# A graph layer that gathers its neighbours: each list gather counts itself when issued, and waits for the count of those ahead

## The chip, the cores and the metric

The kernel runs on one core of a Trainium2 chip. Four engines compute: TensorE (PE), VectorE (DVE), ScalarE (ACT) and GpSimd (POOL); SyncE (SP) issues the plain transfers. GpSimd issues the indirect transfers, those whose rows are picked by a list of indices. The metric is the device time of one execution in microseconds; the number given is the median of the runs.

## The reference, cut to what matters

There are 16 graphs of 1024 nodes with 64 features each and an adjacency matrix for each graph. Per graph, features are normalised and clipped at zero. Nodes with more than ten neighbours lose some edges by a rule on the rank of each neighbour. Then every node takes three quantiles over its remaining neighbours (itself among them), channel by channel, adds their weighted sum to its own features, and a small two-layer network follows.

```python
h = jnp.maximum(_layernorm(x, axis=-1), 0.0)
# inside the layer, x is h
rem = neigh & (sk > 1) & (rank % sk == sk - 1) & mask[:, :, None]
rem = rem | jnp.swapaxes(rem, 1, 2)
adj_d = jnp.where(rem, 0.0, adj_)
nd = adj_d > 0
vals = jnp.where(nd[..., None], x[:, None, :, :], jnp.inf)
s = jnp.sort(vals, axis=2)
...                                   # quantiles 0.25, 0.5, 0.75 with weights 0.25, 0.5, 0.25
out = (1.0 + EPS_GIN) * x + agg
h = jax.nn.relu(out @ W1 + b1)
y = h @ W2 + b2
return y * mask[..., None].astype(y.dtype)
```

The layer's result is added to the original `x`.

## The kernel before

Graphs are worked on in pairs, eight pairs in all. For one graph b, `load` (line 894) brings in the adjacency matrix in eight blocks of 128 rows and turns it into 0/1 form; `number`, `drop` and `keep` find which edges stay; `order` ranks the nodes by their number of neighbours, so that nodes with many stand in the first of eight tiles; `collect` (line 1069) makes, for each node, the list of its neighbours' row numbers, in the tile `idx` (written for the last time at line 1134). `normalize` writes the normalised features to a table in HBM, `gtab`.

`fetch` (line 1263) then gathers. One list gather is one indirect transfer: for one slot s of one tile k it brings 128 rows of 64 floats, one row for each node of the tile, from `gtab` into a slot of the tile `g` of its class. There are four classes of tiles (`CLASSES`: tile 0; tiles 1 to 3; 4 and 5; 6 and 7); classes with tiles 0 to 3 have two buffers, the other two have one. A pair has at most 126 such gathers, the last pair fewer, since part of its lists is fetched by matrix products (`pick`, line 1313). There are 952 list gathers in all. `fetch_group` (line 1606) issues 30 more indirect transfers for the few nodes with very long lists, and `scatter` (line 1688) four that write results; the change does not touch these.

`aggregate` (line 1435) sorts the gathered slots by a network of minima and maxima on DVE (lines 1376 to 1384), weights them, and adds them up on PE (line 1405). It reads the `g` tiles, so a later gather into the same buffer must wait for it. `mlp` is the small network.

The kernel's text creates the instructions in one order, and `arrange` (line 643) makes another. It takes each instruction as a step with an estimated cost, works out which steps must precede which, and runs a list scheduler: at each point the engine that is free first takes the earliest step that is ready. The result is one sequence for each engine, fixed when the program is built. Waits between engines are put in afterwards by the framework. Every indirect transfer adds 16 to one of eight semaphores when its data has landed, and the ninth waits on the semaphore of the first, and so on; so at most eight are under way.

In the built program, an instruction carries one wait. Where it has to wait for more, EventSemaphore instructions stand in front of it on the same engine, which do nothing but wait, for one or two semaphores each.

GpSimd runs its sequence in order. It has 986 indirect transfers in it, and they come in some twenty bursts: at the head of each stands a gather that waits for its list (`idx`, from DVE), or for the buffers of `g` (from PE, ACT and DVE).

The lines around the change:

Of the kernel before, what the change touches and what calls it, by code (L numbers as in the profile page):

```python
# [639 lines left out]
        return 480, 1500 + by / 300  # L640


def arrange(tc, runs, loose, tails):

    steps, found, number = [], {}, {}
    for ins in list(tc.nc.cur_bb.bb.instructions):
# [58 lines left out]
    waiting, able, sequence = ({e: [] for e in ENGINES} for _ in range(3))  # L705
# [4 lines left out]
    while done < len(steps):  # L710
# [5 lines left out]
        s = steps[heappop(able[e])]  # L716
# [19 lines left out]
        for q in ENGINES:  # L736
            while waiting[q] and waiting[q][0][0] <= free[q]:
                heappush(able[q], heappop(waiting[q])[1])

    for steps in sequence.values():  # L740
        alike = iter(sorted((i for s in steps for i in s.tail), key=lambda i: number[i.name]))
        line = [i for s in steps for i in (s.ins, *(next(alike) for _ in s.tail))]
        at = {ins.name: k for k, ins in enumerate(line)}
        for ins in line:
            if ins.name in loose and at[loose[ins.name]] < at[ins.name] - 1:
                tc.declare_no_dep(ins, loose[ins.name], reason="read in order by one engine")
        for ins, then in zip(line, line[1:]):
            tc.add_manual_dep(
                then, ins.name, mybir.DependencyInfo(mybir.DependencyClass.NoSync, mybir.DependencyReason.DATA),
                reason="order of the engine",  # L750
            )
# [3 lines left out]
def list_layer(  # L755
# [14 lines left out]
    nc = tc.nc  # L770
# [8 lines left out]
    runs = []  # L779
# [15 lines left out]
    loose, tails = {}, {}  # L795
# [95 lines left out]
    lists, owns, coefs, tables = {}, {}, {}, {}  # L891
# [348 lines left out]

    queue = deque()
    turn = [0]

# [9 lines left out]
    def opening(some, m=B // 2 - 1):  # L1255

        tiles, slots = some
        if (m, tiles) not in gathered:
            gathered[m, tiles] = wk.tile(
                [P, PLANS[slots][0], len(tiles), 2, C], F32, name=f"g{tiles[0]}", bufs=2 - tiles[0] // 4  # L1260
            )

    def fetch(m, classes=CLASSES, halves=(0, 1)):

        for tiles, slots in classes:
            lo, n = tiles[0], len(tiles)
            held, order = PLANS[slots][:2]

            def begin(h, tiles=tiles, lo=lo, n=n, slots=slots, held=held):
                opening((tiles, slots), m)  # L1270
                nc.scalar.copy(gathered[m, tiles][:, slots - 1, :, h], owns[m][:, lo:lo + n, h])

            def gather(h, slot, k, at, tiles=tiles, lo=lo):
                return nc.gpsimd.indirect_dma_start(  # L1274
                    out=gathered[m, tiles][:, slot, k - lo, h], out_offset=None, in_=tables[2 * m + h][0],
                    in_offset=bass.IndirectOffsetOnAxis(ap=lists[2 * m + h][:, at:at + 1], axis=0),
                    element_offset=tables[2 * m + h][1],
                )

            for h in halves:  # L1280
                queue.append(partial(begin, h))
                for k in tiles:
                    for s, slot in enumerate(order[:FULL[k] + ((k, FULL[k]) in HOSTS)]):
                        if m < pairs - 1 or s >= LEAST[k]:
                            queue.append(partial(gather, h, slot, k, PASSED[k] + s))
# [149 lines left out]
    def aggregate(m, o, between=None):  # L1435
# [4 lines left out]
        for half in (0, 1) if last else (1, 0):  # L1440
            parts = CLASSES[2 * half:2 * half + 2][::1 if last else -1]
            for sides in ((0, 1), (1, 2)) if last and half else ((0, 2),):
# [47 lines left out]
                if half and not last:  # L1490
                    for h in ((0, 1),) if m < pairs - 2 else ((0,), (1,)):
                        fetch(m + 1, CLASSES[2:], halves=h)
# [272 lines left out]
    late_constants()  # L1765
    drain(ahead, drop(0), normalize(0), keep(0), order(0), collect(0, ((0, 1), (1, NT))))
    fetch(0, halves=(0,))
    issue()
    drain(load(1), prepare(1))
    fetch(0, halves=(1,))  # L1770
    issue()
    for m in range(pairs + 1):
# [22 lines left out]
                next(side)  # L1795
        weave(chain(results(m - 1) if m else (), (1.0,)), 140.0 if m else 1.0, side, 85.0 if m < pairs - 1 else 45.0)

    arrange(tc, runs, loose, tails)


def ones_col(pool, nc):
# [68 lines left out]
@with_exitstack  # L1870
def quantile_graph_layer(
    ctx: ExitStack,
    tc: tile.TileContext,
    x: bass.AP,
    adj: bass.AP,
    nodemask: bass.AP,
    W1: bass.AP,
    b1: bass.AP,
    W2: bass.AP,
    b2: bass.AP,  # L1880
    cbf: bass.AP,
    cf32: bass.AP,
    ci32: bass.AP,
    out: bass.AP,
):
    keep = ctx.enter_context(tc.tile_pool(name="keep", bufs=1))
    flag = keep.tile([1, 1], I32, name="flag")
    list_layer(tc, x, adj, nodemask, W1, b1, W2, b2, cbf, cf32, out, flag)
    full = tc.nc.values_load(flag[0:1, 0:1], min_val=0, max_val=1)
    with tc.If(full > 0):  # L1890
        dense_layer(tc, x, adj, nodemask, W1, b1, W2, b2, cbf, cf32, ci32, out)
# [83 lines left out]
```

## Time and profile before

| | |
|---|---|
| runs | 1517.57 us median of 3 (1513.0 to 1521.52) |
| profiled execution | 2610.97 us, of which the span from first to last instruction is 2609.2 us |
| busy in the span | DVE 1224.7 us, PE 1220.6, ACT 1111.4, POOL 966.4 |
| list gathers (line 1274) | 952, 921.0 us busy, 967 ns on average, 942 to 1491 |
| other indirect transfers | 26 and 4 at lines 1624 and 1628, 4 at line 1691: 33.2 us busy |
| granted clock of PE | 0.709 of full speed |
| moved by DMA | 121.62 MB, 47 GB/s |

Busy time is the time in which an engine has at least one instruction in work; waiting, branches and the sequencer's own work are not in it. [...] The profiled execution is a run with recording on, and it took 1.72 times as long as the runs without; so its durations of single instructions can be used, but its sums of idle time have to be read with care.

### The profile page before, as it was taken

How to read it: one execution, taken by the hardware profiler on the slowest of the kernel's cores; microseconds unless marked ns; L12 is line 12 of the kernel's file. 1: busy time of each engine (PE TensorE's matmuls, PEld its weight loads, DVE VectorE, ACT ScalarE, POOL GpSimd, SP SyncE). 2: the span in 40 equal slices, each digit the busy share in tenths (PEclk: the TensorE clock that was granted, in tenths of full speed). 3: DMA queues.
4: the chain of work that ended last, by engine and by line, in shares of the span. 5: the costliest groups of instructions: out<-in, count | busy, mean ns of one | idle time of the engine just before them, and what ended most of it. 6: DMA issues, size and time to landing. Idle time of an engine off the chain costs nothing.

```text
span 2609.2 us, 29583 instructions
## 1 busy us (share of the span) xinstructions
PE 1220.6 (47%) x8971; PEld 756.3 (29%) x8971; DVE 1224.7 (47%) x5963; ACT 1111.4 (43%) x3089; POOL 966.4 (37%) x995
## 2 busy tenths in 40 slices
PE   6144246154807192253816427145392254655536
PEld 4133134032404151142413214033251122353223
DVE  5123168043508371383507704088374171449496
ACT  6244146143606271343606626055482254315355
POOL 1724431653272527324370154702507434420400
PEclk9567578576958595585957758577596566876668
DMA  5222122121213121221212112121212010100100
GB/s 171 62 77 68 39 56 73 33 58 45 56 34 86 28 70 32 62 52 50 59 26 80 42 19 59 26 65 33 51 54 50 16 21 16 32 13 3 22 9 11
DMA packets 128826, 121.62 MB, mean 47 GB/s; under 512 B 95730, under 2 KB 96274, under 8 KB 128658
## 3 DMA queue, kind: packets, MB, share of 16 engines
q1 hardware_dynamic: 97106, 87.29, 11.3%
q0 software_dynamic: 31552, 32.36, 6.4%
q8 instruction: 72, 1.18, 0.2%
q14 instruction: 96, 0.79, 0.1%
HBM read 108.79 MB, written 9.05 MB: 45 GB/s over the span
## 4 chain that ended last, share of the span: by engine, by line
another core or an unknown queue 27%; PE 17%; ACT 17%; issue 16%; DVE 6%; DMA 0%; DVEq 0%; ACTq 0%
PE codeP L1090 3%; PE acc L1405 3%; ACT dist L993 2%; ACT g L1399 2%; ACT kept L1016 2%; ACT sg L906 2%; DVE g L1384 1%; ACT ne L926 1%; PE tp L913 1%; DVE g L1379 1%; PE rk L988 1%; PE rk L983 1%; PE got L1341 1%; ACT waste L1188 1%
## 5 line engine op out<-in xcount | busy, mean ns | idle before, releaser
L1274 POOL DMA_INDIRECT g<-gtab,idx x952 | 921.0, 967 | 1373.9 <-issue 307.7
L1384 DVE TENSOR_TENSOR g<-g 128x256 f32<-128x256 f32 (+1 forms) x675 | 312.0, 484 | 39.0 <-remote 26.6
L1379 DVE TENSOR_TENSOR g<-g 128x256 f32<-128x256 f32 (+1 forms) x675 | 312.8, 486 | 28.8 <-remote 18.9
L993 ACT ACTIVATE dist<-rk,bias 128x512 f16<-128x512 f32 x256 | 170.2, 696 | 314.4 <-remote 215.0
L983 PE MATMUL rk<-kb,cnt 128*128 128x512 bf16 x256 | 121.4, 474 | 349.0 <-ACT dist L993 166.9
L926 ACT ACTIVATE ne<-tp 128x512 fp8e4<-128x512 f32 x248 | 141.0, 605 | 280.3 <-remote 226.3
L994 DVE TENSOR_SCALAR rem<-dist,half 128x1024 bf16<-128x1024 f16 x128 | 63.0, 493 | 402.6 <-ACT dist L993 351.7
L913 PE MATMUL tp<-kb,sg 128*128 128x128 bf16 x1024 | 118.4, 258 | 285.2 <-ACT sg L906 114.7
L988 PEld LDWEIGHTS <-ne 128*128 128x128 fp8e4 x1024 | 97.7, 117 | 414.4 <-issue 396.9
L1090 PE MATMUL codeP<-pack,perm 128*128 128x332 bf16 x1024 | 195.1, 333 | 11.2 <-DVE perm L1065 8.7
L913 PEld LDWEIGHTS <-sg 128*128 128x128 bf16 x1024 | 89.5, 118 | 309.0 <-issue 172.1
L1016 ACT ACTIVATE kept<-kp 128x512 fp8e4<-128x512 f32 x224 | 134.2, 615 | 91.8 <-remote 54.1
L1405 PE MATMUL acc<-g,kf 128*128 128x128 f32 (+2 forms) x472 | 141.2, 432 | 64.5 <-ACT g L1399 45.3
L1399 ACT ACTIVATE g<-g,coef 128x64 f32<-128x64 f32 x560 | 147.5, 350 | 52.2 <-DVE g L1379 21.0
L801 DVE MEMSET pause<- 128x1 bf16 x2237 | 132.0, 59 | 7.0 <-issue 7.0
L988 PE MATMUL rk<-kw,ne 128*128 128x128 fp8e5 x1024 | 128.7, 258 | 0.0
L906 ACT ACTIVATE sg<-at 128x1024 bf16<-128x1024 f32 x121 | 126.5, 1070 | 3.4 <-DMA at<-in_adj_dram 3.4
L1105 DVE MAX8 keys<-codeP 128x8 f32<-128x128 f32 x128 | 38.0, 297 | 186.7 <-ACT own L1100 145.1
L1090 PEld LDWEIGHTS <-perm 128*128 128x128 bf16 x1024 | 97.2, 105 | 89.3 <-DVE perm L1065 25.1
L1511 DVE TENSOR_SCALAR at_p<-iota,node 128x512 bf16<-128x512 f16 x208 | 66.8, 357 | 100.0 <-remote 57.4
L1019 PE MATMUL code<-kw,kept 128*128 128x17 fp8e5 x1024 | 65.5, 173 | 98.9 <-issue 56.6
L1405 PEld LDWEIGHTS acc<-g,kf 128*128 128x128 f32 x472 | 83.4, 218 | 90.0 <-ACT g L1399 57.1
(205 smaller groups left out, 2533.5 us busy)
## 6 DMA issues: line engine op xcount, KB each, us to landing
at<-in_adj_dram SPq DMA_DIRECT2D x122, 512.0 KB
g<-gtab,idx POOLq DMA_INDIRECT x952
xt<-in_x_dram SPq DMA_DIRECT2D x16, 256.0 KB
y<-in_x_dram SPq DMA_DIRECT2D x16, 256.0 KB
gtab<-xt SPq DMA_DIRECT2D x16, 256.0 KB
out_dram<-y SPq DMA_DIRECT2D x14, 256.0 KB
spare<-in_adj_dram SPq DMA_DIRECT2D x6, 512.0 KB
gg<-g SPq DMA_DIRECT2D x32, 48.0 KB
```

What stands on the lines that cost most here:

```text
L906: nc.scalar.activation(sg, at, AF.Sign)
L913: run.append(nc.tensor.matmul(tp[:, s], sg[:, m * P:(m + 1) * P], ident16, start=(s == 0), stop=(s == 3 and t // 4 != n), skip_group_check ...
L926: nc.scalar.activation(to, tp, AF.Relu, saturate=False)
L988: run.append(nc.tensor.matmul(rk[:, s * P:(s + 1) * P], ne[:, 4 * n + s, ts], upper, start=False, stop=(s == 3), skip_group_check=True,))
L993: nc.scalar.activation(dist[:, n * HALF:(n + 1) * HALF], rk, AF.Abs, bias=bias[:, t:t + 1])
L1016: nc.scalar.activation(kept[:, 4 * n:4 * n + 4], kp, AF.Relu, saturate=False)
L1090: run.append(nc.tensor.matmul(flat, perm[:, t, k * P:(k + 1) * P], pack[:, t], start=False, stop=(t == NT - 1), skip_group_check=True,))
L1274: return nc.gpsimd.indirect_dma_start(out=gathered[m, tiles][:, slot, k - lo, h], out_offset=None, in_=tables[2 * m + h][0], in_offset=bas ...
L1379: nc.vector.tensor_tensor(at(f + k * df, df, many), pa, pb, OP.min if what == "<" else OP.max)
L1384: nc.vector.tensor_tensor(pa if back else pb, pa, pb, OP.max if what == "<" else OP.min)
L1399: nc.scalar.activation(v[:, i, j], v[:, i, j], AF.Copy, scale=w[:, i, j:j + 1])
L1405: nc.tensor.matmul(acc, ident32, lines[:, s], start=False, stop=(s == now[-1] and not ends), skip_group_check=True)
```

## The change

One semaphore, `issued`, is allocated. Each list gather adds one to it when GpSimd has finished with the instruction[...]; the data may land later. After the scheduler has fixed GpSimd's sequence, `arrange` walks over the list gathers in that sequence and makes the gather with number k (counted from zero, from the third on) wait until the semaphore has reached k - 1: all gathers in front of it but the last have been issued. Nothing else changes: data, sizes and the order of the instructions on all engines stay as they are.

```diff
-def arrange(tc, runs, loose, tails):
+def arrange(tc, runs, loose, tails, paced):
...
+    for k, s in enumerate(s for s in sequence["POOL"] if s.ins.name in paced[1]):
+        if k > 1:
+            paced[1][s.ins.name].wait_op(paced[0], k - 1, "sem-ge")
     for steps in sequence.values():
...
+    paced = nc.alloc_semaphore("issued"), {}
     queue = deque()
...
+            issued, given_out = paced
+
             def gather(h, slot, k, at, tiles=tiles, lo=lo):
-                return nc.gpsimd.indirect_dma_start(
+                ins = nc.gpsimd.indirect_dma_start(
                     out=gathered[m, tiles][:, slot, k - lo, h], out_offset=None, in_=tables[2 * m + h][0],
                     in_offset=bass.IndirectOffsetOnAxis(ap=lists[2 * m + h][:, at:at + 1], axis=0),
-                    element_offset=tables[2 * m + h][1],
+                    element_offset=tables[2 * m + h][1], engine_sem=issued,
                 )
+                given_out[ins.ins.name] = ins
+                return ins
...
-    arrange(tc, runs, loose, tails)
+    arrange(tc, runs, loose, tails, paced)
```

In the built program, 950 gathers wait on `issued`. The wait takes the one place that an instruction has, so what the gather waited on before moves into EventSemaphore instructions in front of it; GpSimd has 136 of these before and 1048 after.

## The prediction

> **What bounds the kernel now.** I read the totals of the engines first, then the row of the list gathers, then GpSimd in order of time.
>
> The head of the page, with its second part's rows for the two engines that matter here:
>
> ```profile
> span 2609.2 us, 29583 instructions
> ...
> PE 1220.6 (47%) x8971; PEld 756.3 (29%) x8971; DVE 1224.7 (47%) x5963; ACT 1111.4 (43%) x3089; POOL 966.4 (37%) x995
> ...
> DVE  5123168043508371383507704088374171449496
> ...
> POOL 1724431653272527324370154702507434420400
> ```
>
> Two things stand out. Four engines are busy for about the same time, 966 to 1225 us. And the profiled execution took 2610.97 us where the runs have a median of 1517.57: the slices say where the rest is, since where POOL has a 7, DVE has a 0 or 1. The table of stretches shows one long run of gathers (565 to 600) beside a stretch without any; its columns are length, then busy time of PE, weight loads, DVE, ACT and POOL, clock and DMA:
>
> ```profile
> 565.00:600.00 35.00, 0.40 (x2) 0.00 (x0) 0.00 (x0) 0.00 (x0) 26.50 (x28) 0.56 0.14 26
> ...
> 200.00:223.00 23.00, 16.60 (x136) 11.11 (x135) 17.34 (x83) 14.60 (x46) 0.00 (x0) 1.00 0.27 81
> ```
>
> While gathers are issued back to back, PE, DVE and ACT nearly stand still, in the profiled execution. The plain runs can hold little of that: they are 1093 us shorter, and at 1517 us the three engines must be working through the gathers. So I take the rates of single instructions from this trace, and not its idle times.
>
> The gathers' own rate is in their group row and in order of time (start, duration, and in brackets the idle time before):
>
> ```profile
> L1274 POOL DMA_INDIRECT g<-gtab,idx x952 | 921.0, 967 | 1373.9 <-issue 307.7 <-ACT o L1418 307.7 <-DVE idx L1134 251.0
> ```
>
> ```profile
> 223.11 0.95 POOL L1274 DMA_INDIRECT g<-gtab,idx  x1 [74.28 <-DVE idx L1134]
> 224.36 0.95 POOL L1274 DMA_INDIRECT g<-gtab,idx  x1 [0.30 <-issue]
> ...
> 549.63 0.95 POOL L1274 DMA_INDIRECT g<-gtab,idx  x1 [0.30 <-issue]
> 550.89 1.28 POOL L1274 DMA_INDIRECT g<-gtab,idx  x1 [0.30 <-issue]
> ```
>
> A gather takes 0.946 us beside an idle DVE and, over the 149 gathers beside which DVE was busy at least 80% of the time, 1.064 on average; 0.305 us lie between two, whatever they waited for. In a plain run DVE is busy some 80% (1224.7 of 1517), so one gather costs about 1.25 to 1.37 us, and the 986 indirect transfers 1234 to 1350. Before the first stand 69.7 us and after the last 57 (2609.2 less 2552.3). That leaves 41 to 157 us of the median for waits at the heads of the 20-odd bursts. GpSimd is therefore the bound or next to it: what is added to every gather shows nearly in full, what is added at a burst's head in part.
>
> [...] the first gather's record starts at 69.74 and its last semaphore increment comes at 72.1, 1.2 us after the record's end. [...]
>
> **The change, part by part.** The order of instructions is the same on all engines, and the waits of PE, ACT, DVE and SP are the same too. On POOL, 952 gathers get an increment, 950 a wait on the new semaphore. An instruction holds one wait, so what it held before goes into an EventSemaphore ahead of it: 136 become 1048.
>
> *The new wait.* Gather k may go when k-2 is issued[...]. It has the 1.25 us of k-1 to arrive. What GpSimd's sequencer must do in that time: one EventSemaphore, 0.086 us from one to the next in a row of them at 1957.5; the gather itself, 0.52 to 0.57 us from the EventSemaphores before it to those behind it (two cases there); and from the release of a wait to the start of the gather 0.26 us (below). Together 0.9 us, less than 1.25: hidden under gather k-1, and the spacing stays. The cover is gone only if a gather became shorter than 0.9 us, or the increment came more than some 0.35 us late.
>
> *The EventSemaphores.* 912 times 0.086 us is 78 us of the sequencer's time, all in that cover. In the trace 36 indirect transfers already have EventSemaphores ahead of them inside a burst, up to four, and 35 of them start 0.305 us after their predecessor like the rest.
>
> *The heads of the bursts.* Here there is no gather to hide under. Queued behind a waiting head are only the other gathers; for these wait the sorts of the next pair. Before, the last wait of a head stood in the gather itself[...]. From the release to the start it took 0.26 us at 15 heads: idx is written at 222.58 + 0.27 and the gather starts at 223.11.
>
> ```profile
> 222.58 0.27 DVE L1134 SCALAR_TENSOR_TENSOR idx<-bit,low 128x104 int32<-128x104 f32 x1
> ```
>
> Now this wait is in an EventSemaphore[...]. Five heads (at 1485.38, 1809.93, 2123.63, 2210.87 and 2406.43) already end their wait in an EventSemaphore: from PE's increment to the start 0.727 us each, 0.697 of it behind the EventSemaphore. So 15 heads lose 0.47 us, 7.0 us, and the five pay one more EventSemaphore, 0.09 each, 0.4 us. At most 7.5 us.
>
> *The increment.* No row shows a gather with one. It costs nothing if it goes out while the next begins (the matrix engine and DVE do so hundreds of times)[...]. It can't make a gather shorter, but fewer waiting gathers could help others, which is the second rival. I take nothing.
>
> *Sum.* In the profiled execution 7.5 us at most, 2611 to 2618. In the runs a head counts where GpSimd really waits there; I take two thirds, 5 us: 1517.57 + 5 = 1522.6, +0.3%.
>
> **The rivals.**
> *GpSimd takes longer per gather.* The increment, or one that arrives late, lengthens the spacing. If it came only as the data lands, 2.35 us after the start, two gathers would take 2.35 + 0.26 = 2.6 us, 1.30 instead of 1.25 each: again 0.05, and 48 us in all where GpSimd is the bound. For it: no gather with an increment is in the trace. Against it: 0.35 us of room, and with DVE busy the spacing is already 1.37. From about 0.01 us per gather, 9.5 us, it decides; 0.03 to 0.05 give 1550 to 1570.
>
> *The other engines are freed.* In the profiled execution the standstill goes with queued gathers: in burst after burst the increment of a short PE group comes 9 to 14 us after its matmuls, as if behind some ten gathers. If the cause is how many gathers stand in GpSimd's queue, two in place of six or more take most of it away. A place in the records is this wait of ACT for matmuls that had ended at 559.2:
>
> ```profile
> 600.30 0.60 ACT L926 ACTIVATE ne<-tp 128x512 fp8e4<-128x512 f32 x1 [40.93 <-remote]
> ```
>
> If a tenth to a fifth of DVE's idle 293 us in a plain run (1517.6 less 1224.7) comes of it, the gain is 29 to 58 us: 1460 to 1490. Against it: the runs are 1093 us shorter than the profiled execution, so the standstill looks like a price of recording; standstills go on 5 to 8 us behind the last gather of a burst, when nothing is queued; and a burst keeps its rate, so if the cause is the issuing itself nothing is gained. This is the rival on the other side; it decides when over 12.6 us of standstill in the runs depend on the queue.
>
> *It does nothing.* If GpSimd comes late to most heads in a plain run, even the 5 us vanish: 1517.
>
> **How the numbers follow.** A difference under 0.5% (7.6 us) can hardly be told from none here. Chances: heads delayed, with or without effect, 0.50 (1517 to 1527, likeliest 1523; about a quarter of it over 1525.2); longer spacing 0.25 (1527 to 1612, mostly 1550 to 1570); engines freed 0.20 (1460 to 1510); nothing at all 0.05. Faster: 0.20. Within: 0.37 and 0.05, 0.42. Slower: 0.13 and 0.25, 0.38. For 8 in 10 I leave out the better part of the freed engines' case and the far end of the longer spacing: 1490 to 1565. The likeliest case has 1517 to 1527 of its own.
>
> **What would show it.** In the changed kernel's trace: gathers still 0.30 us apart and 0.946 us long beside an idle DVE; heads that start 0.7 us after their release instead of 0.26; a profiled time of 2600 to 2620. Wrong would be: gaps of 0.35 or more in mid-burst (first rival), or stretches of gathers in which PE, DVE and ACT work (second), with a profiled time hundreds of us shorter.

## The result, and the profile after

The changed kernel takes 1518.44 us (median of 12 runs, 1516.55 to 1524.3), the kernel before 1518.81 (12 runs, 1513.0 to 1524.55). The ratio is 1.0002, with a 95% interval from 0.9986 to 1.0018: no difference. Forecast were 1523 us, with 0.42 on "within 0.5%". The 5 us (+0.3%) of that forecast lie beyond the upper end of the interval.

The profiled execution is another matter: 2610.97 us before, 1518.3 after. The page of the changed kernel:

```profile
span 1516.2 us, 30478 instructions
...
PE 1124.8 (74%) x8954; PEld 711.8 (47%) x8971; DVE 1230.8 (81%) x5963; ACT 1099.1 (72%) x3089; POOL 1031.4 (68%) x995
...
DVE  5646699985899899876994689797899578998984
...
POOL 3177777677777777777777777777777777776000
...
ACT 30%; PE 23%; issue 19%; POOL 14%; DVE 10%; DMA 3%; POOLq 0%; DVEq 0%; SPq 0%; ACTq 0%
...
L1280 POOL DMA_INDIRECT g<-gtab,idx x952 | 983.5, 1033 | 347.9 <-DMA g<-gtab,idx 284.2
```

The busy times are nearly those of before (DVE 1230.8 against 1224.7, ACT 1099.1 against 1111.4), but the span is 1093 us shorter. POOL has a 7 almost everywhere, and DVE works beside it. The row of shares is the chain of work that ended last, followed back from the end: GpSimd has 14% of it. The table of stretches, for the two windows shown of before (the same times, not the same work; length, then busy time of PE, weight loads, DVE, ACT, POOL, then clock and DMA):

```profile
565.00:600.00 35.00, 24.95 (x295) 16.92 (x292) 34.89 (x193) 28.35 (x57) 27.08 (x27) 0.89 0.44 130
200.00:223.00 23.00, 11.26 (x99) 7.95 (x102) 22.03 (x102) 19.66 (x45) 17.75 (x18) 0.78 0.36 104
```

In the first, 27 gathers went out and DVE was busy for 34.89 of 35 us; before, 28 gathers went out and PE, DVE and ACT did next to nothing. I count stretches of over 3 us in which none of PE, ACT and DVE works: 71 with 747 us in all before, none after. The wait of 40.93 us on ACT, at line 926, has no successor either. What that line (now 929) waited for in the whole span, in us and times:

```profile
its engine sat idle before it (us, times) until:
  PE tp L922: 8.8, 8
  PE tp L916: 5.8, 9
```

GpSimd and one line of DVE, in order of time:

```profile
271.35 0.25 DVE L1137 SCALAR_TENSOR_TENSOR idx<-bit,low 128x104 int32<-128x104 f32 x1
272.34 1.04 POOL L1280 DMA_INDIRECT g<-gtab,idx  x1 [8.23 <-issue]
273.68 1.13 POOL L1280 DMA_INDIRECT g<-gtab,idx  x1 [0.30 <-DMA g<-gtab,idx]
...
366.23 0.94 POOL L1280 DMA_INDIRECT g<-gtab,idx  x1 [0.30 <-DMA g<-gtab,idx]
368.01 1.05 POOL L1280 DMA_INDIRECT g<-gtab,idx  x1 [0.84 <-DMA g<-gtab,idx]
369.37 1.07 POOL L1280 DMA_INDIRECT g<-gtab,idx  x1 [0.30 <-DMA g<-gtab,idx]
...
594.29 1.08 POOL L1280 DMA_INDIRECT g<-gtab,idx  x1 [0.30 <-DMA g<-gtab,idx]
595.67 1.08 POOL L1280 DMA_INDIRECT g<-gtab,idx  x1 [0.30 <-DVE g L1392]
```

Three readings. Gathers still stand 0.305 us apart (973 of the 985 gaps). The head at 272.34 starts 0.74 us after its list is written (271.35 + 0.25), not 0.26. And this is the only list gather after the first that waits for over a microsecond: from 69.5 us to the last at 1396.5, GpSimd runs through. The sum of the span is therefore 69.5 us of lead-in, 951 spacings of 1.395 us on average (32 other indirect transfers, 30 of them of `fetch_group`, are among them), and 120 us after the start of the last list gather.

So the range forecast for the runs held, and that of the profiled execution (2600 to 2620 us) failed by over 1080 us. The experiments had two questions: what makes the standstill, and what sets the time where there is none.

### The profile page after: what moved, and what is told of

The parts are those of the page before. It is cut to its first block, busy times and chain, and to the rows that moved or that the text cites. A ratio compares the mean times of both kernels' runs of the same rounds, so it can differ in the third digit from the quotient of the medians.

```text
span 1516.2 us, 30478 instructions
## 1 busy us (share of the span) xinstructions
PE 1124.8 (74%) x8954; PEld 711.8 (47%) x8971; DVE 1230.8 (81%) x5963; ACT 1099.1 (72%) x3089; POOL 1031.4 (68%) x995
## 4 chain that ended last, share of the span: by engine, by line
ACT 30%; PE 23%; issue 19%; POOL 14%; DVE 10%; DMA 3%; POOLq 0%; DVEq 0%; SPq 0%; ACTq 0%
POOL g L1280 14%; PE codeP L1093 5%; ACT dist L996 5%; PE acc L1413 5%; ACT g L1407 4%; ACT kept L1019 4%; ACT sg L909 3%; ACT ne L929 2%; DVE g L1392 2%; DVE g L1387 2%; PE tp L916 1%; ACT waste L1186 1%; ACT waste L1191 1%; PE rk L986 1%; PE rk L991 1%
## 5 line engine op out<-in xcount | busy, mean ns | idle before, releaser
L1280 POOL DMA_INDIRECT g<-gtab,idx x952 | 983.5, 1033 | 347.9 <-DMA g<-gtab,idx 284.2
L1093 PE MATMUL codeP<-pack,perm 128*128 128x332 bf16 x1024 | 182.1, 316 | 9.0 <-DVE perm L1068 8.5
L986 PE MATMUL rk<-kb,cnt 128*128 128x512 bf16 x256 | 113.1, 442 | 74.5 <-ACT dist L996 69.6
L916 PE MATMUL tp<-kb,sg 128*128 128x128 bf16 x1024 | 109.9, 246 | 72.8 <-ACT sg L909 57.5
L991 PEld LDWEIGHTS <-ne 128*128 128x128 fp8e4 x1024 | 90.7, 110 | 129.9 <-issue 107.4
L916 PEld LDWEIGHTS <-sg 128*128 128x128 bf16 x1024 | 82.6, 112 | 94.5 <-ACT sg L909 63.6
L991 PE MATMUL rk<-kw,ne 128*128 128x128 fp8e5 x1024 | 118.8, 243 | 0.0
L1098 ACT CAST st<-codeP 128x4 bf16<-128x4 f32 x128 | 21.6, 169 | 109.9 <-PE codeP L1093 109.6
L1014 PE MATMUL kp<-kw,rem 128*128 128x128 fp8e5 x1024 | 100.5, 219 | 0.0
L1009 PE MATMUL kp<-ne,kw 128*128 128x512 fp8e4 x256 | 98.7, 386 | 0.8 <-ACT dist L996 0.5
```

The lines of the kernel that those rows point to most:

```text
L916: run.append(nc.tensor.matmul(tp[:, s], sg[:, m * P:(m + 1) * P], ident16, start=(s == 0), stop=(s == 3 and t // 4 != n), skip_group_check ...
L991: run.append(nc.tensor.matmul(rk[:, s * P:(s + 1) * P], ne[:, 4 * n + s, ts], upper, start=False, stop=(s == 3), skip_group_check=True,))
L1093: run.append(nc.tensor.matmul(flat, perm[:, t, k * P:(k + 1) * P], pack[:, t], start=False, stop=(t == NT - 1), skip_group_check=True,))
L1280: ins = nc.gpsimd.indirect_dma_start(out=gathered[m, tiles][:, slot, k - lo, h], out_offset=None, in_=tables[2 * m + h][0], in_offset=bass ...
```

## The experiments

**One fact comes first, since no number below can be read without it.** The chips of these runs are of two kinds. On three of them the kernel before takes 1518 to 1522 us. On two others it takes 2624 us (24 runs, 2615 to 2635) and 2647 us (7 runs), without recording. I call them quick and stalling chips; the runs above have the times of the quick ones, though their chips are not on record. Each chip was used in one batch of runs, so whether this is a lasting property of a chip or one of that time is not shown. Each kernel is compared with the kernel before on its own chip.

| kernel | kernel before there | time | ratio, 95% interval |
|---|---|---|---|
| `count_only` | 2624.03 | 2625.95 | 1.0009 (0.9997 to 1.0021) |
| `depth8` | 2624.03 | 2634.31, one run | |
| `depth4` | 2624.03 | 2634.87, one run | |
| `depth1` | 2624.03 | 2603.62 | 0.9923 (0.9892 to 0.9954) |
| `thin_before` | 1517.89 | 1445.56 | 0.9515 (0.9484 to 0.9547) |
| `thin_after` | 1517.89 | 1448.33 | 0.9524 (0.9492 to 0.9556) |
| `after_again` | 1520.22 | 1520.18 | 0.9992 (0.9974 to 1.0011) |
| `depth1_again` | 1520.22 | 1518.88 | 0.9994 (0.9981 to 1.0008) |
| `longer` | 1520.22 | 1516.64 | 0.9983 (0.9970 to 0.9995) |
| `longer2` | 2646.74 | 2201.46 | 0.8324 (0.8297 to 0.8351) |
| `longer4` | 2646.74 | 1993.39 | 0.7525 (0.7513 to 0.7538) |
| `longer3` | 1522.18 | 1824.69 | 1.1992 (1.1972 to 1.2012) |

### Does the number of queued gathers make the standstill?

Four kernels ran on one chip. `count_only` has the increment and no wait:

```diff
-        if k > 1:
-            paced[1][s.ins.name].wait_op(paced[0], k - 1, "sem-ge")
+        pass
```

> The gathers keep their increment of the semaphore, but none waits on it. Theory (the standstill under recording comes from several gathers standing in GpSimd at once, and plain runs don't have it): profiled execution back at 2500 to 2700 us, with PE, DVE and ACT idle in the bursts; plain runs 1512 to 1525 us. Rival (the increment itself, which gives GpSimd a semaphore of its own to signal, is what ends the standstill): profiled execution stays at 1510 to 1530. Rival (a gain and a loss cancel in plain runs): without the waits the runs leave 1518 by more than 8 us.

`depth8` lets eight gathers be unissued, `depth4` four, and `depth1` only the one that waits:

```diff
-        if k > 1:
-            paced[1][s.ins.name].wait_op(paced[0], k - 1, "sem-ge")
+        if k > 7:
+            paced[1][s.ins.name].wait_op(paced[0], k - 7, "sem-ge")
```

> Gather k waits until all in front of it but the last seven have been issued. The transfers' own eight semaphores allow no more than that anyway, so the wait never holds anything back, but nearly as many EventSemaphore instructions stand on GpSimd as in the changed kernel. Theory (number of queued gathers): profiled execution 2500 to 2700 us, plain time 1512 to 1525. Rival (the EventSemaphore between two gathers gives the others room, whatever it waits for): profiled execution 1510 to 1600.

```diff
+        if k > 3:
+            paced[1][s.ins.name].wait_op(paced[0], k - 3, "sem-ge")
```

> Gather k waits until all in front of it but the last three have been issued: up to four in GpSimd instead of two. Theory: profiled execution between the two kernels' if the standstill grows with the number queued, 1600 to 2300 us; if it needs a full queue, 1510 to 1530. Plain time 1512 to 1525 in either case. Rival (EventSemaphores): 1510 to 1530 as with depth two and with depth eight.

```diff
+        if k > 0:
+            paced[1][s.ins.name].wait_op(paced[0], k, "sem-ge")
```

> Gather k waits until all in front of it have been issued: nothing runs on GpSimd while the next gather is released and started. Theory (GpSimd's spacing of gathers sets the time, and with depth two the wait lies under the gather ahead): the spacing grows from 1.34 us by the way from one gather's end to the next one's start, at least 0.26 and at most 0.73 us in place of 0.305, so by 0 to 0.43 us, likeliest 0.3; plain runs longer by 0 to 400 us, likeliest 200 to 280, and by as much as the spacing in the trace says (spacing times 950). Rival (the heads of the bursts or the other engines bound, spacing does not): with a spacing longer by 0.2 us or more the runs stay within 1% of 1518. If the spacing stays the same, the run says that the wait is not paid even without cover.

All four took 2604 to 2635 us, and so did the kernel before beside them in plain runs; of `depth8` and `depth4` there is only the profiled execution. The theory's 2500 to 2700 for the profiles of `count_only` and `depth8` was met, but not for its reason, and its range for `depth4` was missed. It also ends the statement that all these expectations shared, that plain runs don't have the standstill: 2624 us is the plain time of the kernel before on this chip. Recording doesn't make it: the profiled execution of `count_only` took 2626.54 us beside a median of 2625.95, and that of `depth1_again` below 1519.15 beside 1518.88.

The strictest of the four, `depth1`, from its page:

```profile
span 2604.6 us, 30495 instructions
...
DVE  5123168062507372192606804078375080529596
...
POOL 1724431644262416515271153700606515340500
```

and `count_only` in the table of stretches, in the window shown above for the changed kernel:

```profile
565.00:600.00 35.00, 0.00 (x0) 0.00 (x0) 0.00 (x0) 1.03 (x3) 25.75 (x28) 0.50 0.13 26
```

Where POOL has a 7, DVE has a 0 or 1, although at most one gather at a time can be in work. The stretches without PE, ACT and DVE sum to 775 us in `count_only`, 830 in `depth8`, 826 in `depth4`, 785 in `depth1`. So the number of gathers queued on GpSimd isn't the cause, and neither the increment nor the EventSemaphores are a cure. Nor is PE's lower clock, 0.705 there against 0.872 in the changed kernel's profile: its busy time is 1226.9 us in `count_only` against 1124.8, which is 102 us of some 1100. (The gap of `depth1` stays at 0.305 us: its wait costs nothing there even without cover.) What these kernels don't limit is the number of transfers that have left GpSimd and not yet landed. The 0.8% by which `depth1` is faster there stays unexplained.

### Where is the changed kernel on a stalling chip?

The changed kernel once more, without an edit:

> The changed kernel as it is. The kernel before took 2624 us on one chip, without recording, and 1518 on another; whichever of the two kinds of chip this is, the theory (the standstill belongs to the chip, and neither recording nor the number of queued gathers makes it) expects the changed kernel within 1% of the kernel before, 2600 to 2640 us or 1510 to 1526. Rival (pacing to two ends the standstill where it is): on a chip where the kernel before takes 2624 us, the changed kernel takes 1520 to 2400.

This run was on a quick chip: 1520.18 us against 1520.22. It repeats the result, but doesn't tell the rival apart. The changed kernel itself has not run on a stalling chip; depth two lies between depth one and depth four, which both stand still there, and I infer the rest.

### What does the wait cost when nothing covers it?

The edit is that of `depth1`, on a quick chip.

> Each gather waits for all in front of it. On the chip with the standstill the gap between two gathers stayed at 0.305 us. Theory (the gap of 0.305 us is itself the way from the end of one gather to the release of the next, so that a wait for the whole of it costs nothing more): gap 0.305 us, time within 0.7% of the kernel before. Rival (it has no cover and costs 0.1 us or more per gather where the other engines work): gap over 0.4 us, over 1560 us on a chip where the kernel before takes 1518.

The time is 1518.88, ratio 0.9994. The gap is 0.305 us, 973 times; theory right. GpSimd around a longer gap, in order of time:

```profile
366.95 0.94 POOL L1280 DMA_INDIRECT g<-gtab,idx  x1 [0.30 <-DMA g<-gtab,idx]
369.98 0.94 POOL L1280 DMA_INDIRECT g<-gtab,idx  x1 [2.08 <-issue]
371.22 0.95 POOL L1280 DMA_INDIRECT g<-gtab,idx  x1 [0.30 <-DMA g<-gtab,idx]
```

The semaphore records say why the gap doesn't grow: the increment of `issued` comes 10 ns after the gather's end, and the next gather starts 0.29 us after it. This is the gap itself; what GpSimd does in it is in no record.

The exception has a period. Each 106th of GpSimd's gathers is followed by a gap of about 2.09 us with depth one, and of 0.51 to 0.84 with depth two; `count_only`, `thin_before`, `depth4` and `depth8` have none. (`longer`, below, has 0.54 to 0.81 us there, with its memsets in between.) 2.09 less one gather with its gap, 1.25, is 0.84: as if something here took some 2.1 us, of which one gather ahead can cover 1.25. That it is one and the same piece of work is argued from the period and the difference; what it is, no record says. `thin_after`, below, with 144 gathers fewer, has the longer gaps at the same counts, so they go with the number of transfers and not with a place in the work. In the changed kernel this costs GpSimd 3.1 us in eight places, in `depth1_again` about 15 us in nine, and neither is seen in the runs: in `depth1_again` the last list gather starts 12.8 us later than in the changed kernel (1409.2 against 1396.5), and 108 us remain behind it instead of 120. So GpSimd has slack.

### Is GpSimd what bounds the kernel on a quick chip?

`thin_before` and `thin_after` leave 144 list gathers out:

```diff
+            def blank(h, end, tiles=tiles):
+                nc.vector.memset(gathered[m, tiles][:, 0:end, :, h], 1.0)
+
             for h in halves:
                 queue.append(partial(begin, h))
+                if tiles[0] == 6:
+                    queue.append(partial(blank, h, slots - 1))
+                    continue
```

> The kernel before, with the 144 list gathers of tiles 6 and 7 left out; their slots are filled with a constant by 16 memsets on DVE of some 0.7 us each, so sorts and sums work on other values, and the output is another. Theory (GpSimd's gathers set the time): 144 x 1.34 = 193 us less, less what DVE (1231 us busy in all, plus 11 for the memsets) then holds back: 1330 to 1400 us. Rival (the other engines or waits at the heads set the time): less than 60 us gained, over 1455 us.

It took 1445.56 us, 72 less than the kernel before: between theory (1330 to 1400) and rival (over 1455), nearer the rival. The page:

```profile
span 1442.7 us, 29324 instructions
...
PE 1118.3 (78%) x8956; PEld 703.7 (49%) x8971; DVE 1228.6 (85%) x5979; ACT 1093.2 (76%) x3089; POOL 887.0 (61%) x851
```

The last list gather starts at 1264.7 us, 132 earlier than in the changed kernel, but the end comes only 73 earlier: 178 us remain behind it instead of 120. DVE is busy 85% of the span. So gathers matter, but GpSimd alone doesn't set the time: the 13 us more of `depth1_again` cost nothing, and 132 us less bring 73. The chain that ended last agrees: GpSimd has 14% of it in the changed kernel, 2% in `after_again`, 7% in `depth1_again` and 4% here, and ACT and PE together have 52 to 62%. GpSimd stands next to the bound. (Leaving gathers out also takes away the waits for their data and buffers; the run doesn't separate the two.)

The same edit in the changed kernel is `thin_after`:

> The changed kernel, with the same 144 list gathers left out. GpSimd now has 144 x 1.34 = 193 us of slack more, and so reaches more heads of bursts before their lists and buffers are ready. Theory (a head that is really waited for starts up to 0.47 us later, and that is all that the wait costs): slower than the thinned kernel before by 0 to 7.5 us, likeliest 2 to 5. Rival (the number of queued gathers slows the other engines in plain runs too, and this is only hidden while GpSimd bounds): faster than the thinned kernel before by over 7 us. Rival (nothing at all): within 1.5 us.

1448.33 us against 1445.56. The means of the two kernels' six runs differ by 1.9 us, with an interval of -0.5 to 4.2 (worked out from the runs): theory's 2 to 5 and the rival's "nothing" can't be told apart by time, but "faster by over 7 us" is excluded. In the traces the later start of a head can be seen. The same head, first in `thin_before`, then in `thin_after`, DVE's write of the list and GpSimd's gather:

```profile
268.93 0.25 DVE L1134 SCALAR_TENSOR_TENSOR idx<-bit,low 128x104 int32<-128x104 f32 x1
269.44 0.94 POOL L1274 DMA_INDIRECT g<-gtab,idx  x1 [5.79 <-DVE idx L1134]
```

```profile
271.31 0.25 DVE L1137 SCALAR_TENSOR_TENSOR idx<-bit,low 128x104 int32<-128x104 f32 x1
272.30 1.05 POOL L1280 DMA_INDIRECT g<-gtab,idx  x1 [5.00 <-issue]
```

From DVE's increment to the start the semaphore records have 0.259 us and 0.727 us, the same at five heads: 5 x 0.47 = 2.3 us. The other seven of the longer gaps add 3.4 us to GpSimd, most of it covered.

`longer` and its sisters add to every gather. The kernel before gets one memset on GpSimd behind each list gather (`longer`); `longer2`, `longer3` and `longer4` get two, three and four. The memsets go along with their gather and count for nothing in the scheduler, so that the other engines keep their order (here `longer2`):

```diff
-            at.busy += 12
+            at.busy += 0 if ins.engine == mybir.EngineType.Pool else 12
...
-    pause = cst.tile([P, 64], BF16, name="pause")
+    pause = cst.tile([P, 32], BF16, name="pause")
+    rest_of = cst.tile([P, 1, 32], BF16, name="rest_of")
...
+                for _ in range(2):
+                    then = nc.gpsimd.memset(rest_of[:, 0], 0.0)
+                    tails[then.ins.name] = ins.ins.name
```

> The kernel before, with a memset of 128 x 32 bf16 on GpSimd behind each list gather, into a tile that nobody reads; nothing else is moved. A memset of 128 x 1 takes 0.10 us in the trace of before, so a gather's spacing should grow by 0.1 to 0.2 us. Theory (on a chip without the standstill GpSimd's gathers set the time, and what is added to each is paid in full): 952 x 0.1 to 0.2 = 95 to 190 us more, 1610 to 1710. Rival (GpSimd is only one of several bounds, as the 72 us gained by leaving out 144 gathers say: 0.37 of their time): 35 to 70 us more, 1553 to 1590. Rival (it is hidden): within 10 us of 1518. On a chip with the standstill, the idle GpSimd (37% busy) would take it for nothing: 2600 to 2650.

Theory and first rival missed, and the rival "it is hidden" held: nothing was added. GpSimd of `longer` in order of time:

```profile
601.19 0.14 POOL L1280 MEMSET rest_of<- 128x32 bf16 x1
601.50 1.06 POOL L1275 DMA_INDIRECT g<-gtab,idx  x1 [0.17 <-issue]
602.55 0.34 POOL L1280 MEMSET rest_of<- 128x32 bf16 x1
602.86 1.31 POOL L1275 DMA_INDIRECT g<-gtab,idx  x1
```

The memset lies inside the gap, and the gap stays at 0.305 us, even where the memset takes 0.34 and ends just after the next gather's start. So the run said nothing of GpSimd's weight, and that its interval ends just under 1 (1516.64 us) is too little to build on. Three memsets reach beyond the gap:

> The kernel before with three memsets behind each list gather. Gaps were 0.305, 0.470 and 0.834 us with one, two and four of them, so about 0.65 with three, and a gather's spacing 1.66 to 1.71 us. From the first of 986 at 69 us the last then starts at 69 + 985 x 1.66 to 1.71 = 1704 to 1753 us at the earliest. On a chip where the kernel before takes 1518 us: theory (the spacing is paid, less the slack behind the last list gather, which is 108 to 123 us there and 58 where GpSimd alone sets the end): 1704 to 1753 + 58 = 1762 to 1811 us; rival (GpSimd bounds without slack): 1518 + 952 x 0.345 = 1846 or more. On a chip where it takes 2647 us: theory (the standstill comes when gathers are closer than some 1.5 us, and is gone with more room): 1762 to 1900, under the 1993 of four memsets, where GpSimd sets the time; rival (the standstill only shrinks in step with the memsets): near the middle of 2201 and 1993, 2050 to 2130.

On a quick chip: 1824.69 us, 302.5 more than the kernel before. Its page:

```profile
span 1823.0 us, 32422 instructions
...
POOL 2488888888888888888887888888888888887880
...
POOL 60%; issue 15%; PE 8%; ACT 8%; DMA 5%; DVE 3%; SPq 0%; DVEq 0%; POOLq 0%; ACTq 0%
```

The median gap is 0.652 us, as expected, but the mean is 0.708, which I had left out, so the time lies 14 us over the theory's 1762 to 1811; the rival needed 1846, so both missed, the theory by less. The limit of some 1.5 us in the expectation's other half was my estimate; no run tests it. The last list gather starts at 1771.2 instead of 1396.5, +375 us, and behind it 52 us remain instead of 120. So a longer spacing is paid in full, less some 68 us of slack behind the last gather. Here GpSimd does set the time: it has 60% of the chain.

### What ends the standstill on a stalling chip?

> The kernel before, with two memsets of 128 x 32 behind each list gather. One memset (0.14 us) fitted into the gap of 0.305 us and cost nothing. Two take 0.28, and with the 0.17 us that followed the one the gap should be about 0.45 us: +0.14 per gather, 138 us in all. Theory (GpSimd's gathers set the time in full): +100 to 140 us, 1620 to 1660. Rival (one bound of several, slope 0.37 as with the 144 gathers left out): +40 to 60 us, 1560 to 1580. Rival (the gap stays at 0.305 us, since the next gather's 0.3 us run beside the memsets): within 8 us of 1519, and nothing learned of the slope.

> The same with four memsets, 0.56 us, gap 0.6 to 0.75 us: +0.3 to 0.45 per gather, 285 to 430 us over 952. Theory (GpSimd sets the time): the time grows by 80 to 100% of (spacing added) x 952, 1770 to 1950 us, since the more GpSimd takes, the less of it can hide. Rival (slope 0.37): 1625 to 1680. Rival (hidden): within 8 us of 1519.

They ran on a stalling chip, and the expectations, worked out for a quick one, were all missed: 2201.46 and 1993.39 us where the kernel before takes 2646.74. The same work with *more* of it on GpSimd is 17% and 25% faster. From the pages, first `longer2`, then `longer4`:

```profile
span 2192.4 us, 31470 instructions
...
DVE  5415188433645763475646505558666814179896
...
POOL 2673862878386847838682475822807887710700
```

```profile
span 1998.3 us, 33374 instructions
...
DVE  5542757924578467756764536677467563674895
...
POOL 2488878888888888778887888788888888888770
```

and GpSimd of `longer4` in order of time:

```profile
600.82 0.95 POOL L1275 DMA_INDIRECT g<-gtab,idx  x1
601.77 0.68 POOL L1281 MEMSET rest_of<- 128x32 bf16 x4
602.61 0.95 POOL L1275 DMA_INDIRECT g<-gtab,idx  x1
```

In `longer4` POOL has a 7 or 8 from the third slice to the 39th, and DVE works beside it: gathers and memsets follow each other from 69.5 to 1940.7 us with no gap between gathers over 2.3 us, one gather every 1.9 us on average, and GpSimd sets the time. In `longer2` five of POOL's 7s and 8s still meet a 0 or 1 of DVE.

A better measure than idle stretches is how late PE's semaphore increments come. For each recorded increment I took the time since the end of the last matmul in front of it; 13 or 14 ns is the median everywhere.

| kernel | gap between gathers, us | chip | increments over 2 us late | sum of those over 1 us late, us | DMA increments in the trace |
|---|---|---|---|---|---|
| before (the profile shown) | 0.305 | see below | 97 | 1229 | 5832 |
| `count_only` | 0.305 | stalling | 103 | 1307 | 5753 |
| `depth1` | 0.305 | stalling | 108 | 1414 | 5785 |
| `longer2` | 0.470 | stalling | 90 | 468 | 7762 |
| `longer4` | 0.834 | stalling | 7 | 48 | 14112 |
| after | 0.305 | quick | 3 | 21 | 20145 |
| `longer3` | 0.652 | quick | 3 | 20 | 20292 |

(Not every increment of PE is recorded: of 1322, the traces of `longer2` and `longer4` have 1182 and 1109, the others 1274 to 1314.) On a stalling chip the lateness goes as gathers are spread out; on a quick chip there is hardly any even at 0.305 us. ACT's and DVE's increments are seldom late: 2 and 19 by over 2 us in the profile of before. So with the gathers spread out by memsets the standstill ends. That the rate at which they leave is what counts is argued, with two rivals left: a gather's data land over 2 us after its start (its first increment comes 2.1 to 2.5 us after it in the stretch below), so a lower rate also leaves fewer transfers under way at once, and the memsets come together with the room (one memset in an unchanged gap was not run on a stalling chip). Gathers themselves aren't late there: at 222 to 235 us in the profile of before, those of their increments that are recorded begin 2.1 to 2.5 us after each start, one gather every 1.25 us. What differs besides is the last column. Of the 15,776 increments that 986 indirect transfers make, 16 each (each of the first three in the changed kernel's trace has all 16), the profile of before holds 2389, `longer2` 5163, `longer4` 10,986, and that of the changed kernel 15,593. Whether the increments are merged or only not recorded, and whether they are what holds up PE's, no run here tells; and what makes a chip stalling stays open as well.

The first row also tells what the profile of before was: its time, its slices and its lateness are those of a stalling chip, while the 1517.57 us beside it have the time of a quick one, and so has the profile of the changed kernel. Hence the 1093 us between the two profiled executions are put down to the chips and not to the change; the chip of either profile is not on record.

## Why the prediction was right, and where it was wrong

*GpSimd is the bound or next to it.* Next to it, and the part "what is added to every gather shows nearly in full" is wrong at this point. In the changed kernel's trace the gathers run from 69.5 to 1396.5 us without a real wait. I had left 41 to 157 us for waits at the heads of bursts and 57 for the end; the heads wait for 8 us in one place, and 120 us follow the last list gather, 62 to 68 more than where GpSimd alone sets the end (58 in `longer4`, 52 in `longer3`). Beyond that slack an addition is paid: +375 us on GpSimd gave +302. Within it nothing was seen: +13 us in `depth1_again` gave none. In the other direction -132 us gave -73, since other chains, mostly of ACT and PE, come next.

*The new wait is hidden under gather k-1, and the spacing stays.* Right: 0.305 us, 973 times. It even holds with no gather ahead (`depth1_again`), since the 0.29 us from the increment to the start are the gap itself. What I had missed is each 106th gather, 0.2 to 0.5 us, 3.1 us in all.

*The EventSemaphores lie in the cover.* Right: 1008 in the trace, and `depth8`, which has nearly as many, keeps its gap at 0.305 us.

*The heads.* The price was exact: 0.26 us became 0.727. That the wait then stands in an EventSemaphore ahead of the gather is seen in the traces: 96 of these on GpSimd before, 1008 after. Why the start then takes 0.47 us longer, no record shows. The number of heads was wrong. I took two thirds of 7.5 us from the heads of the profile of before; in the changed kernel's trace GpSimd comes late to the heads of all bursts of list gathers but one. The 5 us vanish, which was the mechanism of the rival to which I gave 0.05, and its 1517 us were the nearest number. The forecast held because its range was wide and the missing 5 us were small.

*The increment costs nothing.* Right: it goes out 10 ns after the gather's end, 0.29 us before the next starts, and the gap stays at 0.305 us.

*The rival of longer spacing* (0.25) is excluded by the gap, which is 0.305 us with and without the change. *The rival of the freed engines* (0.20) read the delay as a matter of how many gathers stand queued; that these were six or more was my estimate, which no record shows. `depth1` has one and stands still as before. The argument I gave against it, that a burst keeps its rate and that if the cause is the issuing itself nothing is gained, fits the runs: with the rate kept nothing is gained, and with the rate lowered a stalling chip gains 17 to 25%.

*The step that failed* is the reading of the profile in the first part: "a price of recording". I had 2611 us beside runs of 1517 and took the act of recording as the only difference, so I forecast 2600 to 2620 us for the changed kernel's profile as well. The runs show plain executions of 2624 us, and profiled ones that take no longer than the plain ones beside them, so recording is not the difference. That this error left the forecast of the runs alone was luck in part: the times forecast hold for a quick chip only. Taking rates of single instructions from that trace was sound nevertheless: a gather beside an idle DVE takes 0.946 us there and 0.944 in the changed kernel's trace, and beside a DVE that is busy for at least 80% of it 1.059 there (146 gathers; the prediction's 1.064 is a little high) and 1.055 in the changed kernel's (740). Not every DVE operation does that: in the changed kernel's trace the 35 gathers beside which DVE is as busy with MAX8 and MATCH_REPLACE8 and their value loads alone take 0.943.

## What to carry to other kernels

When a profiled execution is far from the runs, don't explain the difference before the same kernel has been timed on the chip that was profiled. A limit on how many transfers stand queued didn't change the rate at which they leave (0.305 us between two at each depth); where they stalled the other engines, room between them helped (2646.74 us became 1993.39 with four memsets), and where they didn't, the room was paid for once it used up the slack (1522.18 became 1824.69 with three). That an engine runs without a pause doesn't make it the bound: add a little to it and see whether the time moves. A wait that stands in the waiting instruction itself and is fulfilled by the one ahead cost nothing here (the gap stayed at 0.305 us), but for the gap at each 106th transfer; what it pushes into an EventSemaphore cost 0.47 us at each place where the engine really waits for it, so count those places in a trace without the disturbance.

## What was not expected of the hardware

- Chips of two kinds in these runs: the same program at 1518 to 1522 us on three and at 2624 to 2647 us on two, with PE's increments up to 44 us late on the latter while gathers leave every 1.25 us, and hardly any late when they leave every 1.8 to 1.9.
- A memset of 0.14 us, at times of 0.34, fits into the gap of 0.305 us between two gathers without lengthening it; two make it 0.470, three 0.652, four 0.834.
- Each 106th indirect transfer of GpSimd is followed by a gap of 2.09 us instead of 0.305 when each waits for the one ahead, of 0.51 to 0.84 when it waits for the one before that, and of 0.305 when four or more may stand unissued; the reason isn't known.
